# Two graph layers: layer 0 with values stationary in column halves of the array and masks in DRAM, layer 1 with queries on partitions

## The chip, the cores and the metric

The kernel runs on one core of a Trainium2 chip. Time is device microseconds of one execution; lower is better. A profiled execution gives the trace from which the views below are taken.

## The reference

x is 8 x 2048 x 256 in f32 and adj is 2048 x 2048 of 0 and 1, sparse and the same for all batches. Layer 0 is masked attention with 4 heads of 64, whose softmax runs inside each chunk of 256 keys by itself, so a query sums eight separate softmaxes:

```
h = relu(layernorm(x))
scores = clip(q k^T / sqrt(64), -10, 10);  scores = where(adj == 0, -10, scores)
attn = softmax(scores over the 256 keys of a chunk)
ctx = sum over the 8 chunks of attn @ v
x = x + layernorm(ctx @ Wo^T + bo + h) * gamma + beta
```

Layer 1 is graph attention with one head: the logit of a query n and a key m is a sum of two scalars through a leaky relu, and the softmax runs over all keys.

```
g = relu(layernorm(x)) @ W;  s = g @ a1;  d = g @ a2
e = leaky_relu(s[n] + d[m], 0.01);  e = where(adj == 0, -1e9, e)
x = x + relu(softmax(e over m) @ g)
```

All is f32. Because s[n] is the same for all keys of a query, the largest logit of a query follows from the largest d among its neighbours.

## The kernel before

The eight batches run one after the other, and all loops are unrolled. In each batch four blocks of 512 tokens (`nb`) are loaded, normalized, transposed and projected (`project_qkv`); q and k stay with features on partitions, v with tokens on partitions, and v has a column of ones after each head's 64 (L118). Then the four blocks of queries go through layer 0, and then layer 1 runs over the whole batch.

Layer 0, per query block: `logits` (L226) makes for a head pair `p` and a key tile `mt` of 128 keys the scores with keys on partitions. The two heads lie in the upper and lower 64 rows of the array. One instruction on VectorE (L236) clips and masks them, taking the lesser of the score and `bound` (an int8 mask of keys by queries that lies in SBUF), and ScalarE takes the exponential (L240). `mix` (L243) then takes 128 x 128 pieces of these exponentials as the stationary operand, and the 65 columns of v and ones as the moving one, so that a chunk's weighted values and their sum come out with queries on partitions; VectorE divides (L255, L263), and GpSimd adds the chunk to `ctx4` (L264). A pass of the loop is a head pair and a chunk (two key tiles); `mix` follows one pass behind `logits`.

At a block's end `finish_layer0` (L266) transposes the context, projects it, adds, normalizes and adds to x; `start_layer1` (L304) normalizes again, multiplies by W (with two more columns for s and d), and folds the block's d into `dmax`, the largest d among each query's neighbours, by 16 instructions on VectorE (L326) with a second mask, `far`, also in SBUF.

Layer 1 (L342) has keys on partitions: for each half of the queries and each key tile, ScalarE takes a relu of a row of s plus the key's d (L379), GpSimd adds a row (L382), ScalarE takes the exponential (L383), VectorE masks (L384), and TensorE multiplies by g with eight accumulators that fill all of PSUM (L388). VectorE and GpSimd finish the eight query tiles (L394 to L401), and the block is stored (L404).

PSUM has three tags with two buffers each: `ps_s` of two banks (logits), `ps_a` and `ps_m` of one. The order of the instructions on each engine is not the order of the program text: a planner sorts them by priority (the program order) among those that it takes to be ready, with costs of its own, and each engine then runs them in that fixed order. All transfers go through SyncE's queue.

Of the kernel before, what the change touches and what calls it, by code (L numbers as in the profile page):

```python
# [17 lines left out]
P = 128  # L18
EPS = 1e-5
HEADS = 4  # L20
# [4 lines left out]
TINY = 2.0 ** -60  # L25
FAR = 64.0

NEVER = 1e30
# [3 lines left out]
def gnn_two_layers(  # L32
# [27 lines left out]
    KT = CHUNK // P  # L60
    SC = float(DH) ** 0.5
    assert F == 256 and DH == 64 and N % NB == 0

    const = ctx.enter_context(tc.tile_pool(name="const", bufs=1))
    xpool = ctx.enter_context(tc.tile_pool(name="xpool", bufs=NNB))
# [42 lines left out]
    woT = const.tile([P, FC, F], F32, name="woT")  # L108

    w1s = const.tile([P, FC, F + 2], F32, name="w1s")  # L110
    ones = const.tile([P, 1], F32, name="ones")
    nc.gpsimd.memset(ones, 1.0)

    bound = const.tile([P, NT, N], I8, name="bound")

    far = const.tile([P, NT, N], I8, name="sign")

    v = const.tile([P, NT, HEADS, DH + 1], F32, name="v")  # L118
    g = const.tile([P, NT, F + 1], F32, name="g")
    nc.gpsimd.memset(v[:, :, :, DH:DH + 1], 1.0)  # L120
    nc.gpsimd.memset(g[:, :, F:F + 1], 1.0)

    with tc.tile_pool(name="setup", bufs=2) as setup:
# [10 lines left out]
        for t in range(NT):  # L134
            rows = setup.tile([P, N], I32, tag="rows", name="rows", bufs=3)
            nc.sync.dma_start(rows, adj[t * P:(t + 1) * P, :])
            z = setup.tile([P, N], BF16, tag="z", name="z")

            nc.vector.tensor_scalar(z, rows, 0.0, -2.0, op0=ALU.is_equal, op1=ALU.mult)
            nc.gpsimd.tensor_scalar(far[:, t, :], z, FAR / 2, 0.0, op0=ALU.mult, op1=ALU.add)  # L140
            for half in range(NT // 8):
                pt = ps.tile([P, 8, P], BF16, tag="m", name="ps_z")
                for k in range(8):
                    m = half * 8 + k
                    nc.tensor.transpose(pt[:, k, :], z[:, m * P:(m + 1) * P], ident_b)
                dst = bound[:, half * 8:(half + 1) * 8, t * P:(t + 1) * P]
                if half % 2 == 0:
                    nc.vector.tensor_scalar(dst, pt, CLIP * SC, CLIP * SC, op0=ALU.mult, op1=ALU.add)
                else:
                    nc.scalar.activation(dst, pt, AF.Copy, bias=CLIP * SC, scale=CLIP * SC)  # L150

    nc.sync.dma_start(w1s[:, :, 0:F], w1.rearrange("(c p) f -> p c f", p=P))
# [5 lines left out]
    for c in range(FC):  # L158
        for i, a_r in enumerate((a1_r, a2_r)):
            junk = work.tile([P, F], F32, tag="hn", name="junk", bufs=3)  # L160
            nc.vector.scalar_tensor_tensor(
                junk, w1s[:, c, 0:F], 1.0, a_r, op0=ALU.mult, op1=ALU.mult,
                accum_out=w1s[:, c, F + i:F + i + 1],
            )
# [61 lines left out]
    def logits(pool, q, k, p, nb, mt):  # L226
# [3 lines left out]
        for i in range(2):  # L230
# [4 lines left out]
        e = pool.tile([P, 2, NB], F32, tag="e", name="e", bufs=2 * KT)  # L235
        nc.vector.scalar_tensor_tensor(  # L236
            e, s, -CLIP * SC, bound[:, mt, cols][:, None, :].to_broadcast([P, 2, NB]),
# [5 lines left out]
    def mix(pool, es, ctx4, p, j):  # L243

        for t2 in range(TB // 2):
            a = ps_a()[:, 0:4 * (DH + 1)].rearrange("p (s d) -> p s d", s=4)
            for s in range(4):
                t, i = 2 * t2 + s // 2, s % 2
                for kt in range(KT):
                    nc.tensor.matmul(  # L250
                        a[:, s, :], es[kt][:, i, t * P:(t + 1) * P], v[:, j * KT + kt, 2 * p + i, :],
                        start=kt == 0, stop=kt == KT - 1,
                    )
            rz = small.tile([P, 4], F32, tag="rz", name="rz")
            nc.vector.reciprocal(rz, a[:, :, DH])  # L255
            dst = ctx4[:, 2 * t2:2 * t2 + 2, 2 * p:2 * p + 2, :]
            num = a[:, :, 0:DH].rearrange("p (t i) d -> p t i d", t=2)
            rzb = rz.rearrange("p (t i) -> p t i", t=2)[:, :, :, None].to_broadcast([P, 2, 2, DH])
            if j == 0:
                nc.vector.tensor_tensor(dst, num, rzb, op=ALU.mult)  # L260
            else:
                part = pool.tile([P, 2, 2, DH], F32, tag="part", name="part", bufs=2)
                nc.vector.tensor_tensor(part, num, rzb, op=ALU.mult)  # L263
                nc.gpsimd.tensor_tensor(dst, dst, part, op=ALU.add)  # L264

    def finish_layer0(pool, x4, rn0, ctx4):  # L266

        o4 = pool.tile([P, TB, F], F32, tag="ctx", name="o4", bufs=2)
        for t2 in range(TB // 2):
            pt = ps_m()  # L270
            for i in range(2):
                for c in range(FC):
                    k = i * FC + c
                    nc.tensor.transpose(
                        pt[:, k * P:(k + 1) * P],
                        ctx4[:, 2 * t2 + i, 2 * c:2 * c + 2, :].rearrange("p h d -> p (h d)"), ident,
                    )
            cT = work.tile([P, 2 * FC, P], F32, tag="cT", name="cT")
            nc.scalar.activation(cT.rearrange("p k n -> p (k n)"), pt, AF.Copy)
            pp = ps_m()  # L280
            for i in range(2):
                for c in range(FC):
                    nc.tensor.matmul(  # L283
                        pp[:, i * F:(i + 1) * F], cT[:, i * FC + c, :], woT[:, c, :],
# [19 lines left out]
    def start_layer1(x4, nb, sd, dmax):  # L304
        _, rn = norm_stats(x4)
        hT = normed_transposed(x4, rn)
        for t2 in range(TB // 2):
            pp = ps_s()
            for i in range(2):
                t = 2 * t2 + i  # L310
                for di in range(FC):
                    nc.tensor.matmul(  # L312
                        pp[:, i, 0:F + 2], hT[:, di, t * P:(t + 1) * P], w1s[:, di, :],
# [3 lines left out]
            nc.scalar.activation(g[:, t0:t0 + 2, 0:F], pp[:, :, 0:F], AF.Copy)  # L317
            nc.vector.tensor_copy(
                sd[:, :, t0:t0 + 2].rearrange("p s t -> p t s"), pp[:, :, F:F + 2]
            )  # L320

        far_d = work.tile([P, NB], F32, tag="far_d", name="far_d", bufs=1)
        spread(far_d, sd[:, 1, nb * TB:(nb + 1) * TB], TINY)
        for t in range(NT):
            junk = work.tile([P, NB], BF16, tag="junk", name="junk", bufs=1)
            nc.vector.tensor_tensor_reduce(  # L326
                junk, far[:, t, nb * NB:(nb + 1) * NB], far_d, 1.0,
                -2 * FAR if nb == 0 else dmax[:, t:t + 1], ALU.add, ALU.max, dmax[:, t:t + 1],
            )

    def spread(dst, col, scale=1.0):

        for c4 in range(col.shape[1] // 4):
            pt = ps_m()
            for i in range(4):
                t = 4 * c4 + i
                nc.tensor.transpose(
                    pt[:, i * P:(i + 1) * P], col[:, t:t + 1].to_broadcast([P, P]), ident
                )
            nc.scalar.activation(dst[:, c4 * 512:(c4 + 1) * 512], pt, AF.Copy, scale=scale)  # L340

    def layer1(pool, b, xs, sd, dmax):  # L342
        W = N // 2
        src, dst = sd[:, 0, :], sd[:, 1, :]
        s_r = pool.tile([P, N], F32, tag="s_r", name="s_r", bufs=1)
        spread(s_r, src)
        top = pool.tile([P, 3, NT], F32, tag="top", name="top", bufs=1)
        none, w, zm = (top[:, i, :] for i in range(3))

        part = pool.tile([P, 2, NT], F32, tag="part1", name="part1", bufs=1)  # L350
        low, high = part[:, 0, :], part[:, 1, :]
        nc.vector.tensor_scalar(low, dst, SLOPE, None, op0=ALU.mult)
        nc.vector.tensor_tensor(high, dst, low, op=ALU.subtract)
        w_r = pool.tile([P, N], F32, tag="w_r", name="w_r", bufs=1)
        nc.vector.tensor_scalar(none, dmax, -FAR / 2, None, op0=ALU.is_lt)
        nc.vector.scalar_tensor_tensor(zm, dmax, 1.0 / TINY, src, op0=ALU.mult, op1=ALU.add)
        nc.vector.scalar_tensor_tensor(zm, zm, SLOPE, zm, op0=ALU.mult, op1=ALU.max)
        nc.vector.scalar_tensor_tensor(w, src, SLOPE, zm, op0=ALU.mult, op1=ALU.subtract)

        nc.vector.scalar_tensor_tensor(w, none, -NEVER, w, op0=ALU.mult, op1=ALU.add)  # L360
        spread(w_r, w)

        pg = ps_m()
        for m in range(NT):
            nc.tensor.matmul(
                pg[:, 0:F + 1], ones.to_broadcast([P, P]), g[:, m, :], start=m == 0, stop=m == NT - 1
            )
        gsum = pool.tile([P, F + 1], F32, tag="gsum", name="gsum", bufs=1)
        nc.scalar.activation(gsum, pg[:, 0:F + 1], AF.Copy)  # L369
        for half in range(N // W):  # L370
            cols = slice(half * W, (half + 1) * W)
            accs = []
            for _ in range(2):
                two = ps_s()
                accs += [two[:, 0, 0:F + 1], two[:, 1, 0:F + 1]]
# [88 lines left out]
```

## Time and profile before

| | |
|---|---|
| three runs | 5951.31, 5952.5 and 5953.0 us, median 5952.5 |
| the profiled execution | 5953.0 us, its span 5951.2 us |
| busy: TensorE matmuls, its weight loads | 4897.3 us (82%), 3684.2 us (62%) |
| busy: VectorE, ScalarE, GpSimd | 3133.4 (53%), 2116.9 (36%), 1837.6 us (31%) |
| mean granted TensorE clock | 0.91 |
| HBM read, written | 35.65 MB, 16.78 MB |

A row of the groups reads: line, engine, operation, tile written and tiles read, shapes, count; then the busy time in us and the mean ns of one; then the idle time of the engine just before and what ended it. PE is TensorE's matmuls, PEld its weight loads, DVE is VectorE, ACT ScalarE, POOL GpSimd, SP SyncE. A matmul's recorded duration includes its way through the pipeline, so the distance from start to start is the better price.

### The profile page before, as it was taken

The page shows a single profiled execution, that of the slowest core. Times are in us where ns is not written, and L with a number is a line of the kernel's source. Part 1 is how long each engine was busy: PE and PEld are TensorE (multiplying, and loading weights), DVE is VectorE, ACT ScalarE, POOL GpSimd, SP SyncE. Part 2 cuts the span into 40 slices and gives each one's busy share as a digit, 9 for nine tenths or more (in the row PEclk, how much of TensorE's full clock was granted, in tenths as well). Part 3 has the DMA queues.
Part 4 walks back from the last instruction along what each step waited for, and adds up shares of the span by engine and source line. Part 5 has one row for each costly group of instructions (what it writes and reads, how often), then busy time and mean ns, then how long its engine had stood idle before and what let it go on. Part 6 is the DMA issues. An engine that isn't in the chain of part 4 may idle for free.

```text
span 5951.2 us, 70683 instructions
## 1 busy us (share of the span) xinstructions
PE 4897.3 (82%) x28304; PEld 3684.2 (62%) x28304; DVE 3133.4 (53%) x6245; ACT 2116.9 (36%) x2361; POOL 1837.6 (31%) x1626
## 2 busy tenths in 40 slices
PE   7888698886988779887798777987789877897877
PEld 4666566665666556665666656665566655665656
DVE  4556445554455544555445554455544556445563
ACT  3333343333333243333433334332343333432333
POOL 2222422224222242223522225123251222513235
PEclk7999899998999989998899988998899988998989
DMA  3000000000000000000000000000000000000000
GB/s 142 1 1 1 0 29 1 1 1 11 18 1 1 1 15 15 1 1 1 15 15 1 1 1 15 15 1 1 1 15 15 1 1 1 15 15 1 1 1 15
DMA packets 39191, 56.96 MB, mean 10 GB/s; under 512 B 2000, under 2 KB 36816, under 8 KB 36816
## 3 DMA queue, kind: packets, MB, share of 16 engines
q1 hardware_dynamic: 38864, 52.44, 2.6%
q8 instruction: 225, 3.69, 0.3%
q14 instruction: 102, 0.84, 0.0%
HBM read 35.65 MB, written 16.78 MB: 9 GB/s over the span
## 4 chain that ended last, share of the span: by engine, by line
PE 56%; POOL 16%; DVE 14%; issue 8%; ACT 6%; DMA 0%; POOLq 0%; SPq 0%; ACTq 0%; DVEq 0%
PE ps_a L250 27%; PE ps_s L231 14%; POOL e L382 9%; DVE junk L326 4%; PE ps_m L206 4%; ACT e L379 3%; DVE e L236 3%; PE ps_s L312 2%; PE ps_m L283 2%; PE ps_m L215 2%; PE ps_m L195 1%; DVE e L384 1%; POOL x L302 1%; POOL o L301 1%; POOL o L300 1%
## 5 line engine op out<-in xcount | busy, mean ns | idle before, releaser
L250 PEld LDWEIGHTS ps_a<-v,e 128*128 128x128 f32 x16384 | 1872.2, 192 | 391.8 <-issue 303.2
L250 PE MATMUL ps_a<-v,e 128*128 128x65 f32 x16384 | 1943.6, 276 | 11.2 <-DVE part L263 10.8
L240 ACT ACTIVATE e<-e 128x1024 f32<-128x1024 f32 x1024 | 1082.2, 1057 | 1706.7 <-DVE e L236 1677.3
L264 POOL TENSOR_TENSOR ctx<-ctx,part 128x256 f32<-128x256 f32 x896 | 666.1, 744 | 2923.6 <-DVE part L263 2923.6
L236 DVE SCALAR_TENSOR_TENSOR e<-ps_s,bound 128x1024 f32<-128x1024 f32 x1024 | 1215.6, 1219 | 185.9 <-PE ps_s L231 185.7
L231 PE MATMUL ps_s<-q,k 64*128 64x512 f32 x4096 | 1096.4, 619 | 33.5 <-DVE e L236 33.5
L382 POOL TENSOR_TENSOR e<-e,w_r 128x1024 f32<-128x1024 f32 x256 | 635.6, 2489 | 671.4 <-ACT e L379 449.4
L384 DVE SCALAR_TENSOR_TENSOR e<-bound,e 128x1024 f32<-128x1024 int8 x256 | 374.7, 1464 | 672.6 <-ACT e L383 667.3
L388 PE MATMUL ps_s<-g,e 128*128 128x257 f32 x2048 | 533.4, 405 | 154.8 <-DVE h L394 100.1
L195 PE MATMUL ps_m<-ident,hn 128*128 128x128 f32 x512 | 121.4, 384 | 588.5 <-ACT hn L185 551.5
L231 PEld LDWEIGHTS ps_s<-q,k 64*128 64x128 f32 x4096 | 362.7, 185 | 343.1 <-issue 133.1
L388 PEld LDWEIGHTS ps_s<-g,e 128*128 128x128 f32 x2048 | 405.3, 202 | 252.2 <-DVE h L394 109.1
L255 DVE RECIPROCAL rz<-ps_a 128x4 f32<-128x4 f32 x1024 | 183.2, 181 | 652.3 <-PE ps_a L250 652.3
L383 ACT ACTIVATE e<-e,part 128x1024 f32<-128x1024 f32 x256 | 293.9, 1148 | 583.0 <-POOL e L382 583.0
L195 PEld LDWEIGHTS ps_m<-ident,hn 128*128 128x128 f32 x512 | 70.0, 183 | 654.4 <-ACT hn L185 599.4
L263 DVE TENSOR_TENSOR part<-ps_a,rz 128x256 f32<-128x256 f32 x896 | 378.4, 424 | 85.5 <-DVE rz L255 2.7
L326 DVE CUSTOM_DVE_ANT_0 junk<-sign,far_d,dmax 128x512 bf16<-128x512 int8 x384 | 292.3, 761 | 33.7 <-ACT far_d L340 29.4
L379 ACT ACTIVATE e<-s_r,part 128x1024 f32<-128x1024 f32 x256 | 287.5, 1136 | 61.2 <-PE ps_m L388 61.2
L388 PE MATMUL ps_m<-g,e 128*128 128x257 f32 x1024 | 271.7, 387 | 40.5 <-ACT gsum L369 38.7
L388 PE MATMUL ps_a<-g,e 128*128 128x257 f32 x1024 | 268.2, 383 | 7.1 <-DVE h L394 7.1
L185 ACT ACTIVATE hn<-x,rn 128x256 f32<-128x256 f32 x128 | 66.4, 589 | 550.3 <-DVE rn L179 550.3
L388 PEld LDWEIGHTS ps_m<-g,e 128*128 128x128 f32 x1024 | 194.2, 192 | 75.7 <-ACT gsum L369 41.9
(88 smaller groups left out, 3490.9 us busy)
## 6 DMA issues: line engine op xcount, KB each, us to landing
rows<-in_adj_dram SPq DMA_DIRECT2D x16, 1024.0 KB, 5.3
x<-in_x_dram SPq DMA_DIRECT2D x32, 512.0 KB, 3.9
out_dram<-x SPq DMA_DIRECT2D x32, 512.0 KB, 3.0
raw<-in_L_gnn_Wq_dram SPq DMA_DIRECT2D x1, 256.0 KB, 4.5
raw<-in_L_gnn_Wk_dram SPq DMA_DIRECT2D x1, 256.0 KB, 4.8
raw<-in_L_gnn_Wv_dram SPq DMA_DIRECT2D x1, 256.0 KB, 6.3
raw<-in_L_gnn_Wo_dram SPq DMA_DIRECT2D x1, 256.0 KB, 6.1
w1s<-in_L_gnn_W_dram SPq DMA_DIRECT2D x1, 256.0 KB, 7.0
```

Of the source, the lines that this page charges most:

```text
L231: nc.tensor.matmul(s[:, i, :], k[p][i * DH:(i + 1) * DH, mt * P:(mt + 1) * P], q[p][i * DH:(i + 1) * DH, cols], start=True, stop=True,)
L236: nc.vector.scalar_tensor_tensor(e, s, -CLIP * SC, bound[:, mt, cols][:, None, :].to_broadcast([P, 2, NB]), op0=ALU.max, op1=ALU.min,)
L240: nc.scalar.activation(e, e, AF.Exp, scale=1.0 / SC)
L250: nc.tensor.matmul(a[:, s, :], es[kt][:, i, t * P:(t + 1) * P], v[:, j * KT + kt, 2 * p + i, :], start=kt == 0, stop=kt == KT - 1,)
L263: nc.vector.tensor_tensor(part, num, rzb, op=ALU.mult)
L264: nc.gpsimd.tensor_tensor(dst, dst, part, op=ALU.add)
L326: nc.vector.tensor_tensor_reduce(junk, far[:, t, nb * NB:(nb + 1) * NB], far_d, 1.0, -2 * FAR if nb == 0 else dmax[:, t:t + 1], ALU.add, A ...
L379: nc.scalar.activation(e, s_r[:, cols], AF.Relu, bias=high[:, m:m + 1], scale=1.0 - SLOPE)
L382: nc.gpsimd.tensor_tensor(e, e, w_r[:, cols], op=ALU.add)
L383: nc.scalar.activation(e, e, AF.Exp, bias=low[:, m:m + 1])
L384: nc.vector.scalar_tensor_tensor(e, bound[:, m, cols], 0.0, e, op0=ALU.is_gt, op1=ALU.mult)
L388: nc.tensor.matmul(accs[k], e[:, k * P:(k + 1) * P], g[:, m, :], start=m == 0, stop=m == NT - 1)
```

## The change

Both layers change, and so does the place of the masks.

Setup: `bound` is written to four DRAM tiles, one for each query block, and the second mask, now `signs` (+1 for a neighbour, -1 else), to sixteen, one for each query tile. The column of ones in v and the two additional columns of w1s go.

Layer 0: the loop over a query block goes over key tiles, both head pairs in each. The values are now the stationary operand (64 columns for a head) and the exponentials the moving one, 512 queries long, so the context comes out with features on partitions. The two heads of a pair lie in the two column halves of the array. The sums come from four further matmuls for each key tile, one for each head in a column quarter of 32, with a stationary operand `picks` of ones and zeros that puts each chunk's sums into its own rows of `z`. ScalarE copies a chunk's unnormalized context to `au`. After each half (four chunks), `normalize` copies the sums out, reshapes them through DRAM, takes reciprocals, spreads them to 64 partitions each through DRAM, multiplies, and adds the four chunks on GpSimd. Finishing a block, and layer 1's start for it, is deferred to key tile 6 of the next block (`late`).

Layer 1: queries are on partitions. For each query tile its sign row is loaded, d is masked (VectorE), its largest found (VectorE), two exponentials are taken (ScalarE, one for each slope) and the larger chosen (VectorE); then the tile is transposed in TensorE, copied from PSUM by ScalarE and VectorE, and multiplied by g. s and d come from VectorE (eight for each block).

The core of the diff:

```diff
-    bound = const.tile([P, NT, N], I8, name="bound")
-    far = const.tile([P, NT, N], I8, name="sign")
-    v = const.tile([P, NT, HEADS, DH + 1], F32, name="v")
+    bounds = [dram.tile([P, NT, NB], I8, name=f"bound{i}") for i in range(NNB)]
+    signs = [dram.tile([P, N], I8, name=f"sign{i}") for i in range(NT)]
+    v = const.tile([P, NT, HEADS, DH], F32, name="v")
+    picks = const.tile([P, HALF_J, 32], F32, name="picks")
+    nc.gpsimd.memset(picks, 0.0)
+    for j in range(HALF_J):
+        nc.gpsimd.memset(picks[:, j, j * JR:(j + 1) * JR], 1.0)
...
-        e = pool.tile([P, 2, NB], F32, tag="e", name="e", bufs=2 * KT)
+        e = pool.tile([P, 2, NB], F32, tag="e", name="e", bufs=5)
...
+    def mix(es, acc, z, au, mt):
+        j, kt = mt // KT, mt % KT
+        jj = j % HALF_J
+        for p in range(HEADS // 2):
+            for i in range(2):
+                nc.tensor.matmul(
+                    acc[p][i * DH:(i + 1) * DH, :], v[:, mt, 2 * p + i, :], es[p][:, i, :],
+                    start=kt == 0, stop=kt == KT - 1,
+                )
+        for h in range(HEADS):
+            nc.tensor.matmul(
+                z[32 * h:32 * h + 32, :], picks[:, jj, :], es[h // 2][:, h % 2, :],
+                start=jj == 0 and kt == 0, stop=jj == HALF_J - 1 and kt == KT - 1,
+            )
+        if kt == KT - 1:
+            for p in range(HEADS // 2):
+                nc.scalar.activation(au[p][:, jj, :], acc[p], AF.Copy)
+
+    def normalize(pool, z, au, ctxT, first):
+        zc = pool.tile([P, NB], F32, tag="zc", name="zc", bufs=1)
+        nc.scalar.activation(zc, z, AF.Copy)
+        rows = HEADS * HALF_J
+        C = P // rows
+        zr = pool.tile([P, NB // C], F32, tag="zr", name="zr", bufs=2)
+        zd = dram.tile([rows, NB], F32, tag="zd", name="zd", bufs=2)
+        nc.sync.dma_start(zd, zc[::JR, :])
+        nc.sync.dma_start(zr, zd.rearrange("r (c f) -> (r c) f", c=C))
+        nc.vector.reciprocal(zr, zr)
+        rd = dram.tile([rows, NB], F32, tag="rd", name="rd", bufs=2)
+        nc.sync.dma_start(rd.rearrange("r (c f) -> (r c) f", c=C), zr)
+        for p in range(HEADS // 2):
+            rb = pool.tile([P, HALF_J, NB], F32, tag="rb", name="rb", bufs=2)
+            for i in range(2):
...
+                nc.sync.dma_start(
+                    rb[i * DH:(i + 1) * DH].rearrange("p j n -> p (j n)"),
+                    src.partition_broadcast(DH),
+                )
+            a = au[p]
+            nc.vector.tensor_tensor(a, a, rb, op=ALU.mult)
+            nc.gpsimd.tensor_tensor(a[:, 0:2, :], a[:, 0:2, :], a[:, 2:4, :], op=ALU.add)
...
+        for t in range(NT):
+            src = sd[:, 0, t:t + 1]
+            sg = pool.tile([P, N], I8, tag="sg", name="sg", bufs=3)
+            nc.sync.dma_start(sg, signs[t])
+            d = pool.tile([P, N], F32, tag="d", name="d", bufs=2)
+            nc.vector.scalar_tensor_tensor(d, sg, BIG, dst, op0=ALU.mult, op1=ALU.min)
...
+            nc.vector.tensor_reduce(dmax, d, AX.X, ALU.max)
...
+            for half in range(2):
...
+                nc.scalar.activation(e1, d[:, cols], AF.Exp, bias=b1)
+                nc.scalar.activation(e2, d[:, cols], AF.Exp, bias=b2, scale=SLOPE)
+                nc.vector.tensor_tensor(e1, e1, e2, op=ALU.max)
+                pt = ps_s().rearrange("p a n -> p (a n)")
+                for k in range(8):
+                    nc.tensor.transpose(pt[:, k * P:(k + 1) * P], e1[:, k * P:(k + 1) * P], ident)
+                eT = pool.tile([P, HALF], F32, tag="eT", name="eT", bufs=2)
+                nc.scalar.activation(eT[:, 0:512], pt[:, 0:512], AF.Copy)
+                nc.vector.tensor_copy(eT[:, 512:], pt[:, 512:])
+                for k in range(8):
+                    m = half * 8 + k
+                    nc.tensor.matmul(
+                        acc, eT[:, k * P:(k + 1) * P], g[:, m, :], start=m == 0, stop=m == NT - 1
+                    )
...
             for nb in range(NNB):
...
+                bd = pool.tile([P, NT, NB], I8, tag="bd", name="bd", bufs=2)
+                nc.sync.dma_start(bd, bounds[nb])
+                for mt in range(NT + 1):
+                    if mt < NT:
+                        es = [logits(pool, q, k, bd, p, nb, mt) for p in range(HEADS // 2)]
+                    if ahead is not None:
...
+                        if m % (KT * HALF_J) == 0:
+                            z = ps_m()
+                            au = [
+                                pool.tile([P, HALF_J, NB], F32, tag="au", name="au", bufs=3)
+                                for _ in range(HEADS // 2)
+                            ]
+                        if m % KT == 0:
+                            acc = [ps_a() for _ in range(HEADS // 2)]
+                        mix(ahead, acc, z, au, m)
+                        if m % (KT * HALF_J) == KT * HALF_J - 1:
+                            normalize(pool, z, au, ctxT, half == 0)
+                    ahead = es
+                    if mt == 6 and late:
+                        late.pop()()
```

## The prediction

> **What bounds the kernel now.** I read the page first, then the busy time by stage, then the timeline inside each stage. On the page:
>
> ```profile
> span 5951.2 us, 70683 instructions
> ...
> L250 PEld LDWEIGHTS ps_a<-v,e 128*128 128x128 f32 x16384 | 1872.2, 192 | 391.8 <-issue 303.2
> L250 PE MATMUL ps_a<-v,e 128*128 128x65 f32 x16384 | 1943.6, 276 | 11.2 <-DVE part L263 10.8
> ...
> L231 PE MATMUL ps_s<-q,k 64*128 64x512 f32 x4096 | 1096.4, 619 | 33.5 <-DVE e L236 33.5
> ```
>
> An f32 matmul stands as two records, each with a weight load (1024 calls of logits give 4096). L250 is half of PE's work, and its busy time (1943.6) hardly exceeds that of its weight loads (1872.2): 65 moving columns do not pay for a 128x128 load. Busy time by stage, for batch 1 (start:end, length, then PE, PEld, DVE, ACT, POOL busy, clock, DMA share, GB/s):
>
> ```profile
> 809.00:862.00 53.00, 51.99 (x179) 28.90 (x179) 17.66 (x46) 22.79 (x36) 3.47 (x4) 0.93 0.09 30
> 862.00:973.00 111.00, 96.53 (x644) 73.29 (x642) 57.98 (x109) 34.14 (x35) 31.08 (x36) 0.96 0.00 1
> 973.00:1352.00 379.00, 316.92 (x2076) 238.27 (x2076) 224.52 (x471) 124.32 (x138) 98.46 (x111) 0.92 0.00 1
> 1352.00:1545.00 193.00, 144.08 (x612) 117.14 (x612) 87.79 (x153) 82.66 (x87) 94.31 (x52) 0.87 0.05 16
> ```
>
> These are: projections (53 us), first query block of layer 0, the other three (126.5 us each), layer 1 (193 us). Eight such batches and some 65 us of setup make the span. Timeline of steady layer 0:
>
> ```profile
> 944.39 1.99 PE L231 MATMUL ps_s<-q,k 64*128 64x512 f32 x8
> ...
> 946.31 3.65 PEld L250 LDWEIGHTS ps_a<-v,e 128*128 128x128 f32 x32 [0.76 <-issue]
> 946.31 3.79 PE L250 MATMUL ps_a<-v,e 128*128 128x65 f32 x32
> ```
>
> This repeats every 5.63 us without a hole: PE bounds it, and L250 takes 3.65 of the 5.63. 16 repeats are 90 us; the other 36 of a block are its end:
>
> ```profile
> 957.91 1.99 PE L283 MATMUL ps_m<-woT,cT 128*128 128x256 f32 x8 [0.69 <-ACT cT L279]
> ...
> 970.55 2.34 POOL L302 TENSOR_TENSOR x<-x,o 128x1024 f32<-128x1024 f32 x1
> ...
> 976.87 2.16 PE L195 MATMUL ps_m<-ident,hn 128*128 128x128 f32 x8 [16.96 <-ACT hn L185]
> ```
>
> PE stands still for 17 us behind a chain of DVE and POOL, comes back at half clock (0.72 in the stage 954 to 976), and then shares DVE with L326. Layer 1's steady part:
>
> ```profile
> 1432.40 1.15 ACT L383 ACTIVATE e<-e,part 128x1024 f32<-128x1024 f32 x1 [2.46 <-POOL e L382]
> ...
> 1433.46 1.13 ACT L379 ACTIVATE e<-s_r,part 128x1024 f32<-128x1024 f32 x1
> ...
> 1434.67 2.35 POOL L382 TENSOR_TENSOR e<-e,w_r 128x1024 f32<-128x1024 f32 x1 [2.30 <-ACT e L379]
> ```
>
> A ring ACT, POOL, ACT of 4.65 us per key tile and half; PE needs 16 records at 0.217 = 3.5.
>
> **What the Trainium skill says.** "TensorEngine Tiling (Array Packing)", section Tiling Modes: tiles work independently, and changing the mode drains TensorE. The trace agrees for row tiles: 8 records of two heads take 4 x 0.429, as one head alone would; and 5.63 - 32 x 0.1115 - 4 x 0.429 = 0.35 us is left for two changes of mode. "TensorE: Matmul & The Clock Gate", Part 3: three column tiles of 32 columns gave 2.38x, and matmuls run strictly in program order. No run here shows column tiles; strict order does not fit the overlap of L231's heads, each of which has two passes. Same page, Part 1: an idle PE falls to half clock; here gaps of 5.2 and 17 us were followed by low clock.
>
> **The change, part by part,** per batch unless said.
>
> *Layer 0, PE.* A key tile for all four heads costs 5.63 now. New: logits unchanged, 4 passes x 0.429 = 1.72. Values: four matmuls with 64 stationary columns and 512 moving, two heads side by side in the columns: 4 passes = 1.72 if the halves overlap, 3.43 if not. Sums: four with 32 columns each: 2 passes = 0.86 if all overlap, 3.43 if not. Three mode changes at 0.18: 0.54. Both ends: 4.83 and 9.1 us. I take 4.83, because the row tiles overlap in just this kind of f32 pair and the page gives column tiles a gain near their number. Weight loads hide: 107 ns beside a pass of 429.
>
> *Layer 0, the others.* Per key tile DVE keeps 2 x 1.22 (L236), loses L255 and L263 (1.21 per key tile), and gains per block four multiplies of 128x2048 (2.27 each by L384's rate, bounds 2.2 to 2.6): about 63 us a block with the block end, below PE's 77. ACT: exp 2.11, evictions 0.6, some 51 a block. POOL loses L264, gains some 17 a block. All stay beside PE's matmuls; were PE as fast as 3.9 us a key tile, DVE would be the bound and each of these would count.
>
> *The half's normalization.* zc copy 0.6, three small transfers at 2.1 (the 1 KB row), reciprocal 0.2, 1 MB spread 5.3 (rows' landing; 3.0 to 8 as ends), multiply 2.3, POOL 2.35 + 1.2, and some 2 of waits: 20 us until one of three au buffers is free again. Only one is spare: the next half needs the second after two key tiles (some 9 us), and its copy waits on ACT; the exps of later key tiles stand behind it, DVE and PE wait for those, and the ps_a buffer that it should free keeps PE from the next values. Five e buffers let PE run on some 7 us (logits, head pair 0, sums). I take 5 us lost per half, clock included (0 to 9): 40. All seven DMAs of a half stand in SP's order, with the bd load behind them; that one is needed only a block later.
>
> *Block ends.* Deferred to the next block's sixth key tile, the chain of 17 us and the low clock hide under its matmuls; what stays on PE is about 9 us (8 + 8 matmuls of 256 columns at 0.43, eight transposes) three times, 27. If z keeps one ps_m buffer too long, the hT of a block comes later, which nobody awaits except after block 3. L274, L279, L326 (16 x 0.84 on DVE) go; eight sums for sd on DVE come (8 x 0.5 = 4).
>
> Sum from the projections' end to the last mix: 4 x 16 x 4.83 + 27 + 40 + 4 filling = 380, against 92 + 3 x 126.5 = 471.
>
> *After the last mix.* Now 19 to x4 and 193: 212. New: normalization 20, output projection and norms 19, W1 and sd 16, dst, first d, reduce and exps 12: 67. Then 16 query tiles. DVE per tile: d 2.27, reduce 2.2 (not in the trace; an estimate at L384's rate, 1.1 to 2.4), four small ones 0.8, two max 2.4, two copies 1.38, end 0.55: 9.6. PE: 16 transposes at 0.11, 16 x 0.433: 8.7, plus waits for eT. ACT 5.7. DVE becomes the bound; with buffers of two to three I take 10.5 (9.4 to 12.5), 168. Sum 235, +23. The order is the planner's, so d of the next tile may go ahead of this one's end; if not, see rival 3. sign loads of 256 KB (3 us) are far ahead in three buffers.
>
> *Setup.* Masks go out to DRAM (16 x 256 KB, 4 x 1 MB) and bounds come back: +20 (0 to 40) once. The dropped w1s columns are nothing (1.8 us of DVE, once). w1's matmuls move to ps_m: no price, beside L236.
>
> Sum: 8 x (-91 + 23) + 20 = -524 against the profiled 5953.0 (span 5951.2 and 1.8 around it; the median, 5952.5, is 0.5 lower): **some 5430 us**.
>
> **The rivals.** (1) *Column tiles do not overlap.* Sums and values then take 16 passes in place of 6: +4.29 per key tile, 275 per batch, less the 40 of waits that it covers: 5430 + 8 x 235 = **7310, slower**. It decides from 10 passes per key tile on (68 + 40 us over 64 tiles is 1.7 us, four passes). For it: no trace of a column tile, and twice to four times the moving data at once. Against: L231.
> (2) *They overlap only in program order*: a head's second pass holds the next head's first. 5 passes for the values and 5 for the sums: +1.72, 110 - 40: **5990**, about no change, 5800 to 6400. For it: rows are shared by column tiles, while L231's heads had their own.
> (3) *Layer 1 goes in series*: DVE holds this tile's end before the next d; 15 us a tile (half of the 22 that the whole chain has) in place of 10.5: +72: **6010**. Against: the trace shows L274 ahead of older L250, so the planner moves work forward.
>
> **How the numbers follow.** Main forecast 0.50, own range 5100 to 5850 (T 4.65 to 5.2, waits 0 to 9, layer 1 9.6 to 12); rival 1 0.18; rival 2 0.22; rival 3 0.10. A measurement here tells 0.2% (12 us). Faster: 0.47 + 0.04 + 0.03 = 0.54; same 0.01 + 0.03; slower 0.02 + 0.15 + 0.18 + 0.07 = 0.42. The range 5100 to 6400 leaves out rival 1 and the tails.
>
> **What would show it.** Eight records of the values in about 1.8 us, eight of the sums in 1.0, a steady period near 4.8: right; 2.2 and 2.2: rival 2; 3.5 and 3.5: rival 1. A gap of PE after each half that ends with a release by POOL or by ACT's au copy: the wait on au. Layer 1 between 10 and 12 us per query tile with DVE over 80% busy: right; under 65%: rival 3. No 17 us gap except once per batch. The forecast is wrong if the period in layer 0 exceeds 6.2.

## The result: 0.7% slower, with TensorE as fast as forecast and waiting more

The changed kernel takes 5994.7 us (median of four runs, 5986.5 to 6001.8) against 5952.6; the ratio is 1.0071, with an interval of 1.0053 to 1.0088. Forecast were 5430 us. The number lies beside those of rivals 2 and 3 (5990 and 6010), but neither mechanism was there, as the trace shows.

The names of its lines: L233 logits, L238 clip and mask, L242 exponential, L254 values, L259 sums, L265 ScalarE's copy to `au`, L290 VectorE's multiply of `au` by the spread reciprocals `rb`, L291 to L296 GpSimd's adds of the chunks, L306 the output projection, L174 to L199 the normalizations and the transposes behind them. From the page after (columns as before):

```profile
L233 PE MATMUL ps_s<-q,k 64*128 64x512 f32 x4096 | 1216.6, 653 | 216.7 <-DVE e L238 216.6
L254 PE MATMUL ps_a<-e,v 128*64 128x512 f32 x4096 | 1152.6, 660 | 248.5 <-ACT au L265 248.5
...
L259 PE MATMUL ps_m<-e,picks 128*32 128x512 f32 x4096 | 598.3, 620 | 0.0
```

The old values (L250) were busy for 1943.6 us; new values and sums together for 1751. In exchange the matmuls of layer 0 now wait: 248.5 us for ScalarE's copies, and 216.7 us in front of the logits where it was 33.5. The steady part, from the timeline of the changed kernel (start, length, engine, line, tiles, records):

```profile
1135.81 1.99 PE L233 MATMUL ps_s<-q,k 64*128 64x512 f32 x8
1137.73 1.94 PE L254 MATMUL ps_a<-e,v 128*64 128x512 f32 x8
1139.60 1.06 PE L259 MATMUL ps_m<-e,picks 128*32 128x512 f32 x8
1140.59 1.13 PE L233 MATMUL ps_s<-q,k 64*128 64x512 f32 x4
```

From start to start a key tile takes 4.78 us (1135.81 to 1140.59), where 4.83 were forecast. Eight records of values in 1.94 us and eight of sums in 1.06 us: the column tiles overlap fully. The single records say it too: in the sums at 1139.60 the first passes of all four heads start within 0.02 us, and the second passes 0.45 us later. Busy time by stage of the changed kernel, batch 1 (start:end, length, PE, PEld, DVE, ACT, POOL busy, clock, DMA share, GB/s):

```profile
827.00:880.00 53.00, 51.41 (x160) 25.98 (x161) 14.05 (x30) 24.28 (x39) 1.09 (x2) 1.00 0.12 40
880.00:1026.00 146.00, 129.35 (x602) 38.79 (x600) 69.55 (x72) 62.52 (x76) 31.80 (x18) 0.96 0.16 38
1026.00:1367.00 341.00, 258.48 (x1068) 81.89 (x1068) 153.93 (x226) 122.37 (x157) 98.42 (x57) 0.83 0.20 44
1367.00:1564.00 197.00, 159.84 (x812) 133.35 (x812) 155.90 (x249) 91.42 (x109) 20.95 (x21) 0.93 0.12 39
```

The stages are projections, the first part of layer 0, its rest with the end of block 3, and layer 1. In the third the clock is 0.83, and TensorE is busy for 258 of 341 us in spite of that. Means over batches 1 to 6, read off the traces (us for one batch; "period" is the time from one batch to the next, "layer 0" runs from the start of the projections to the last logits, "block" from one block's last addition to x to the next one's, the mean of the first two such stretches; e1, e2, e6 and e7 are experiments below):

| kernel | period | layer 0 | block | last logits to end of layer 0 | layer 1 |
|---|---|---|---|---|---|
| before | 733.8 | 513.6 | 126 | 27.1 | 192.4 |
| forecast | 665.8 | 429 | 96 | | |
| after | 737.4 | 484.6 | 118 | 52.8 | 197.7 |
| e1 | 683.8 | 430.8 | 103 | 53.0 | 197.7 |
| e2 | 696.5 | 440.2 | 104 | 56.2 | 197.8 |
| e6 | 661.6 | 405.6 | 96 | | |
| e7 | 641.1 | 384.7 | 89 | 56.3 | 197.7 |

(The forecast's 429 is 53 + 380, less 4 for the last mix; its block is 16 x 4.83 + 9 + 2 x 5.) So the changed layer 0 gained 29 us a batch where some 85 were expected, and layer 0's end with layer 1 lost 31.

Three waits stand in a steady block. The first two come at a block's end, in the timeline of the changed kernel (in brackets: idle time before, and its releaser):

```profile
1099.40 2.29 DVE L290 TENSOR_TENSOR au<-au,rb 128x2048 f32<-128x2048 f32 x1 [4.57 <-DMA rb<-rd]
...
1102.88 1.18 PE L233 MATMUL ps_s<-q,k 64*128 64x512 f32 x4 [2.89 <-DVE e L238]
...
1105.62 3.19 POOL L296 TENSOR_TENSOR ctxT<-ctxT,au 128x512 f32<-128x512 f32 x1
...
1108.84 0.60 ACT L265 ACTIVATE au<-ps_a 128x512 f32<-128x512 f32 x1 [4.92 <-POOL ctxT L296]
...
1109.49 1.98 PE L254 MATMUL ps_a<-e,v 128*64 128x512 f32 x4 [5.42 <-ACT au L265]
```

**Wait A**: VectorE stands in its fixed order at L290 until `rb` has landed; the masks L238 of the next key tiles are queued behind it, and TensorE waits for them. **Wait B**: ScalarE stands at the copy to `au` until GpSimd's L296 has read the oldest of the three buffers; `ps_a` stays full, and TensorE stands at the next values. **Wait C** follows at the deferred start of layer 1:

```profile
1143.17 2.34 POOL L325 TENSOR_TENSOR x<-x,o 128x1024 f32<-128x1024 f32 x1
...
1145.54 0.75 DVE L174 BATCH_NORM_STATS2 stats<-x 128x6 f32<-128x256 f32 x2 [6.19 <-POOL x L325]
...
1147.08 1.19 DVE L238 SCALAR_TENSOR_TENSOR e<-ps_s,bd 128x1024 f32<-128x1024 f32 x1
1148.32 2.07 PE L233 MATMUL ps_s<-q,k 64*128 64x512 f32 x2 [6.60 <-DVE e L238]
```

The same chain through GpSimd as before, but now its end stands on VectorE in front of a mask that TensorE needs. From start to start of matmuls, the block has holes of 3.48, 6.06, 7.20 and 4.16 us, 20.9 in all. By the trace's record of the granted clock, half clock sets in still within the holes and lasts 10.2, 13.7 and 6.8 us; 20.7 us of it lie behind the holes' ends, which costs some 10. TensorE's idle time proper in the four holes, 18.5 us, and these 10 make up the 29 us by which a block is longer here than in e7 (118 for 89).

### The profile page after: what moved, and what is told of

Read it like the earlier page. It is cut to its first block, busy times and chain, and to the rows that moved or that the text cites. A ratio compares the mean times of both kernels' runs of the same rounds, so it can differ in the third digit from the quotient of the medians.

```text
span 5993.0 us, 54681 instructions
## 1 busy us (share of the span) xinstructions
PE 4841.2 (81%) x21392; PEld 2273.5 (38%) x21392; DVE 3201.1 (53%) x4645; ACT 2422.3 (40%) x3057; POOL 1238.2 (21%) x797
## 4 chain that ended last, share of the span: by engine, by line
PE 54%; DVE 18%; POOL 13%; DMA 7%; ACT 5%; issue 2%; SPq 0%; POOLq 0%; DVEq 0%; ACTq 0%
PE ps_a L254 13%; PE ps_s L233 12%; PE ps_a L389 10%; PE ps_m L259 6%; DMA rb<-rd 4%; PE ps_m L208 4%; DVE e L238 3%; DVE d L365 3%; POOL au L291 3%; DVE au L290 2%; PE ps_m L335 2%; DVE e L380 2%; DVE st L368 2%; PE ps_m L306 2%; PE ps_m L217 2%
## 5 line engine op out<-in xcount | busy, mean ns | idle before, releaser
L238 DVE SCALAR_TENSOR_TENSOR e<-ps_s,bd 128x1024 f32<-128x1024 f32 x1024 | 1215.8, 1218 | 1198.0 <-PE ps_s L233 1088.5
L242 ACT ACTIVATE e<-e 128x1024 f32<-128x1024 f32 x1024 | 1076.2, 1053 | 1371.1 <-DVE e L238 1359.9
L233 PE MATMUL ps_s<-q,k 64*128 64x512 f32 x4096 | 1216.6, 653 | 216.7 <-DVE e L238 216.6
L254 PE MATMUL ps_a<-e,v 128*64 128x512 f32 x4096 | 1152.6, 660 | 248.5 <-ACT au L265 248.5
L389 PE MATMUL ps_a<-g,eT 128*128 128x257 f32 x4096 | 958.8, 386 | 66.7 <-ACT eT L385 45.5
L389 PEld LDWEIGHTS ps_a<-g,eT 128*128 128x128 f32 x4096 | 761.2, 191 | 215.4 <-ACT eT L385 83.2
L291 POOL TENSOR_TENSOR au<-au 128x1024 f32<-128x1024 f32 x128 | 300.9, 2351 | 2524.7 <-DVE au L290 2429.3
L233 PEld LDWEIGHTS ps_s<-q,k 64*128 64x128 f32 x4096 | 389.8, 195 | 962.4 <-issue 619.2
L254 PEld LDWEIGHTS ps_a<-e,v 128*64 128x64 f32 x4096 | 266.2, 145 | 992.2 <-issue 640.0
L259 PE MATMUL ps_m<-e,picks 128*32 128x512 f32 x4096 | 598.3, 620 | 0.0
L265 ACT ACTIVATE au<-ps_a 128x512 f32<-128x512 f32 x512 | 297.3, 587 | 380.0 <-PE ps_a L254 162.9
L290 DVE TENSOR_TENSOR au<-au,rb 128x2048 f32<-128x2048 f32 x128 | 306.4, 2393 | 188.0 <-DMA rb<-rd 169.9
L380 DVE TENSOR_TENSOR e<-e,e 128x1024 f32<-128x1024 f32 x256 | 310.3, 1217 | 79.3 <-ACT e L379 79.3
L378 ACT ACTIVATE e<-d,st 128x1024 f32<-128x1024 f32 x256 | 291.6, 1139 | 112.5 <-DVE st L371 112.5
L306 PE MATMUL ps_m<-woT,ctxT 128*128 128x256 f32 x512 | 153.1, 451 | 207.1 <-POOL ctxT L296 207.1
L365 DVE SCALAR_TENSOR_TENSOR d<-sg,dst 128x2048 f32<-128x2048 int8 x128 | 312.8, 2449 | 9.6 <-ACT dst L359 9.6
L379 ACT ACTIVATE e<-d,st 128x1024 f32<-128x1024 f32 x256 | 291.5, 1139 | 0.0
```

Of the source, the lines that this page charges most:

```text
L233: nc.tensor.matmul(s[:, i, :], k[p][i * DH:(i + 1) * DH, mt * P:(mt + 1) * P], q[p][i * DH:(i + 1) * DH, cols], start=True, stop=True,)
L238: nc.vector.scalar_tensor_tensor(e, s, -CLIP * SC, bd[:, mt, :][:, None, :].to_broadcast([P, 2, NB]), op0=ALU.max, op1=ALU.min,)
L242: nc.scalar.activation(e, e, AF.Exp, scale=1.0 / SC)
L254: nc.tensor.matmul(acc[p][i * DH:(i + 1) * DH, :], v[:, mt, 2 * p + i, :], es[p][:, i, :], start=kt == 0, stop=kt == KT - 1,)
L259: nc.tensor.matmul(z[32 * h:32 * h + 32, :], picks[:, jj, :], es[h // 2][:, h % 2, :], start=jj == 0 and kt == 0, stop=jj == HALF_J - 1 an ...
L265: nc.scalar.activation(au[p][:, jj, :], acc[p], AF.Copy)
```

## The experiments

**Theory**: these waits of a fixed order, with the low clock behind them, hold what the forecast gave away. **Rivals**: the column tiles' overlap carries less than it seems; layer 1 is what costs; the holes are only covers, and another engine takes over when they go. Ratios are to the kernel before, with intervals; differences are to the changed kernel (5994.7) unless said.

**e1_au4: a fourth au buffer** (and `zc` in `rb`'s slots, for room):

```diff
-tag="au", name="au", bufs=3
+tag="au", name="au", bufs=4
-zc = pool.tile([P, NB], F32, tag="zc", name="zc", bufs=1)
+zc = pool.tile([P, NB], F32, tag="rb", name="zc", bufs=2)
```

> The changed kernel with four au buffers in place of three (to fit, zc takes a slot of rb's tag). Theory of the order (the column tiles are as fast as forecast, 4.78 us per key tile; what is lost per query block are waits of an engine's fixed order, each followed by a low clock): the copy of au on ScalarE no longer waits for GpSimd (L293 and L296), the gaps of 4.2 and 6.1 us in PE per block go with half of their 17 us of low clock, some 18 us x 32 blocks = 570, less what the wait of the multiply for rb takes over: 5450 to 5750 us. Rival (the transfers of the sums set the pace, so a wait removed comes back at the next consumer): within 1% of the changed kernel's 5995, that is 5935 to 6055.

Measured: 5563.3 us, 0.9347 (0.9333 to 0.9361): 431 us less, 54 a batch. The copy no longer waits for GpSimd; in e1's timeline TensorE itself releases it:

```profile
1010.71 0.60 ACT L265 ACTIVATE au<-ps_a 128x512 f32<-128x512 f32 x1 [1.22 <-PE ps_a L254]
```

What is left of TensorE's waits in e1, the two largest (waiting line <- line awaited: us in total, times, longest):

```profile
PE ps_m L306 <- POOL ctxT L296: 208.8, 16, 23.4
PE ps_s L233 <- DVE e L238: 200.1, 78, 6.7
```

The wait of L254 for ScalarE is gone, and the other waits are about what they were (207.1 and 216.6 in the changed kernel). One buffer was worth over ten times the whole loss of the change.

**e8_zc_only: the control**, with `zc` moved and `au` left at three buffers:

```diff
-zc = pool.tile([P, NB], F32, tag="zc", name="zc", bufs=1)
+zc = pool.tile([P, NB], F32, tag="rb", name="zc", bufs=2)
```

> The changed kernel with three au buffers, but zc in a slot of rb's tag as in e1_au4: the other half of e1_au4's edit by itself. If the fourth au buffer made e1_au4's gain, this stays within 1% of the changed kernel's 5995 (5935 to 6055). If the move of zc or the planner's new order made it, it comes near 5563.

Measured: 6000.8 us, 1.0082 (1.0067 to 1.0098). The move alone brings nothing; the buffer made e1's gain.

**e2_hold: layer 1's start held back** behind the mask of key tile 10, three `au` buffers (names shortened here and below):

```diff
 if mt == 6 and late:
-    late.pop()()              # finish_layer0, then start_layer1
+    late[0][0]()              # finish_layer0
+if mt == 10 and late:
+    with tc.issue_after(last_mask):
+        late.pop()[1]()       # start_layer1
```

> The changed kernel, with layer 1's start for a block traced at key tile 10 of the next block and its VectorE instructions queued behind the masking of that key tile; all else as it was. Theory of the order: the gap of 7.2 us (L174 waits for GpSimd's x, L238 stands behind it) and its 13.7 us at half clock go, in three blocks of a batch: some 14 x 24 = 340 us, 5600 to 5750. Rival (GpSimd's chain is needed then in any case, or PE has no work to fill the gap): 5940 to 6010.

Measured: 5689.2 us, 0.9561 (0.9544 to 0.9577): 306 us less, 38 a batch. In e2's timeline VectorE's statistics now start 3.6 us after the end of GpSimd's addition, and without a wait:

```profile
989.78 2.38 POOL L327 TENSOR_TENSOR x<-x,o 128x1024 f32<-128x1024 f32 x1
...
995.76 0.74 DVE L174 BATCH_NORM_STATS2 stats<-x 128x6 f32<-128x256 f32 x2
```

e2's waits of TensorE (its lines stand two later):

```profile
PE ps_a L256 <- ACT au L267: 164.1, 44, 6.8
...
PE ps_s L235 <- DVE e L240: 21.6, 18, 3.5
```

The wait for masks fell from 216.6 to 21.6 us. A block became 14.1 us shorter (118.2 to 104.1), though the hole was one of 7.2: with it went 10.1 us of half clock behind its end (some 5 lost), and the wait for the copies fell too, from 248.5 to 164.1. The edit does two things, tracing the start at key tile 10 and holding it back; no run takes them apart.

**e3_au4_defer: e1 with the reciprocal and the multiply put later**, behind the masks of a key tile one and four or five after the half's end:

```diff
+steps = normalize(pool, z, au, ctxT, half == 0)    # now stops twice
+due += [[1, steps], [4 + half, steps]]
...
+with tc.issue_after(last_mask):
+    next(steps, None)
```

> Four au buffers as in e1_au4, and the reciprocal and the multiply of a half are queued on VectorE behind the masking of the first and of the fourth or fifth key tile after the half's end. Theory of the order: the multiply no longer stands in front of L238 while its rb is on the way; the gap of 3.5 us per block goes too, so all that hangs on the normalization: 22 us x 32 = 710 in all, 5200 to 5450, and clearly below e1_au4. Rival (the transfers set the pace): no better than e1_au4 within 1%.

Measured: 5668.2 us, 0.9518 (0.9503 to 0.9534): 105 us worse than e1, and a miss. With four buffers the wait A that this was to take away was down to 1.7 us (the block of e1 at 950 to 1050), and a late multiply makes a late context. In e3's timeline TensorE stands at the output projection (here L313) until GpSimd has added the second head pair's context:

```profile
1063.69 1.26 POOL L303 TENSOR_TENSOR ctxT<-ctxT,au 128x512 f32<-128x512 f32 x1
1065.01 2.93 PE L313 MATMUL ps_m<-woT,ctxT 128*128 128x256 f32 x6 [2.98 <-POOL ctxT L303]
```

In e3's waits of TensorE, that wait has grown from e1's 208.8 us at 16 places; the 24 new ones are one for each block whose end is deferred:

```profile
PE ps_m L313 <- POOL ctxT L303: 280.1, 40, 23.4
```

**e4_all: e2 and e3 together**, with the diffs of both.

> e2_hold and e3_au4_defer together. Theory of the order: the two add up, a query block takes 86 to 92 us (16 x 4.78 and some 9 for the block's end) in place of 119, 4900 to 5150 us in all, and the clock inside layer 0 stays at 1.0. Rival (a new bound, VectorE at some 63 us per block or the transfers, comes forward): the sum of the two gains is missed by over a third, 5300 or more.

Measured: 5494.8 us, 0.9227 (0.9213 to 0.9241): on the rival's side of what was expected. The block is near 100 us, with e3's wait of L313 in it and, as in e2 (218.9 us, where the changed kernel has 161.9), one at the transposes L197; e4's waits of TensorE:

```profile
PE ps_m L313 <- POOL ctxT L303: 249.3, 40, 19.6
PE ps_m L197 <- ACT hn L187: 220.7, 72, 17.8
```

**e6_au4_hold: e1 and e2 together**, without e3's part.

> e1_au4 and e2_hold together, without the deferral of the multiply that made e3_au4_defer slower than e1_au4. Theory of the order: the gains add up (432 and 306 below the changed kernel): 5257, 5180 to 5330, a block 89 to 94 us. Rival (with one wait gone the other comes forward, as in e4_all): 5400 to 5500.

Measured: 5400.5 us, 0.9071 (0.9058 to 0.9085): 94 us better than e4, so e3's part costs here too, 70 above the upper end of what was expected and at the lower end of the rival's range. e6's timeline shows what was left in a block:

```profile
1043.32 1.58 ACT L187 ACTIVATE hn<-x,rn 128x256 f32<-128x256 f32 x3 [1.32 <-DVE rn L181]
1043.98 0.33 PE L197 MATMUL ps_m<-ident,hn 128*128 128x128 f32 x1 [1.80 <-ACT hn L187]
```

Wait C once more, an engine further on: TensorE has the transposes in front of logits, while `hn` is still on its way through VectorE and ScalarE. There are 24 such holes in e6, of 2.2 to 3.7 us from start to start; after 23 of them, not after the one shown, half clock followed for 3.4 to 10.2 us.

**e7_hold_all: e6 with the start of layer 1 behind finished work on three engines**, VectorE's mask of key tile 10, ScalarE's exponential of 11 and TensorE's logits of 12:

```diff
-if mt == 10 and late:
-    with tc.issue_after(last_mask):
+if mt == 12 and late:
+    with tc.issue_after(mask[10]), tc.issue_after(exp[11]), tc.issue_after(logits[12]):
```

> e6_au4_hold, with ScalarE's and TensorE's part of layer 1's start queued too, behind the exponentials of key tile 11 and the logits of key tile 12. Theory of the order: the 2.4 us in which TensorE stands before the transposes of hn (seen in e2_hold and e4_all) and its 6.8 us of low clock go, some 5 us x 24 = 120 below e6_au4_hold. Rival: what stands behind them in ScalarE's order waits in its place, within 30 us of e6_au4_hold.

Measured: 5234.6 us, 0.8795 (0.8782 to 0.8809): 166 us under e6, where 120 were expected, and 12% under the kernel before. The start is also traced two key tiles later; no run has that alone. One steady block of e7, as a stage:

```profile
1006.00:1096.00 90.00, 89.83 (x430) 28.76 (x430) 59.05 (x83) 48.81 (x63) 31.84 (x20) 1.00 0.23 49
```

TensorE is busy for all of it at full clock, and VectorE and ScalarE have a third and more to spare. e7's waits of TensorE:

```profile
PE ps_s L386 <- DVE e L383: 179.8, 56, 13.5
PE ps_m L309 <- POOL ctxT L299: 177.2, 16, 19.7
PE ps_m L197 <- ACT hn L187: 165.2, 24, 17.7
```

The long ones among these stand at the seam between the layers, once a batch; whether other matmuls could fill it was not tried. Between the first and the last logits of a batch, the sums of the two traces (means of batches 1 to 6) leave little room for another cause: TensorE is idle for 58.8 us in the changed kernel and for 2.3 in e7, and at work under half clock for 65.6 and 0 us (33 lost). That is 89 of the 100 us between the two.

**e9_one_half: e7 with the values of both heads in the lower column half**, so that they cannot overlap. The context is then the sum of two heads, so this kernel leaves out the separate context of each and serves for the time alone; ScalarE copies the lower half into both halves of `au` (not shown):

```diff
-acc[p][i * DH:(i + 1) * DH, :], v[:, mt, 2 * p + i, :], es[p][:, i, :],
-start=kt == 0, stop=kt == KT - 1,
+acc[p][0:DH, :], v[:, mt, 2 * p + i, :], es[p][:, i, :],
+start=kt == 0 and i == 0, stop=kt == KT - 1 and i == 1,
```

> e7_hold_all with the values of both heads of a pair in the same, lower column half of the array, so that they can't overlap; ScalarE copies that half twice. The context is a sum of two heads and not the reference's: this is left wrong for the sake of the time. If the overlap of the column halves is what makes the new layer 0 short: 4 passes of 0.429 us more per key tile, 110 us a batch, 5235 + 880 = 6115 (5900 to 6150, as slower tiles cover some waits; slower than the kernel before or about equal). Rival (something else sets the key tile's period, the overlap is worth little): 5235 to 5500.

Measured: 6066.3 us, 1.0192 (1.0175 to 1.0209): 832 us above e7. e9's timeline, beside that of the steady part above:

```profile
1002.47 1.99 PE L235 MATMUL ps_s<-q,k 64*128 64x512 f32 x8
1004.39 3.65 PE L257 MATMUL ps_a<-e,v 128*64 128x512 f32 x8
1007.97 1.06 PE L262 MATMUL ps_m<-e,picks 128*32 128x512 f32 x8
1008.97 1.99 PE L235 MATMUL ps_s<-q,k 64*128 64x512 f32 x8
```

The values take 3.65 in place of 1.94 us and the period is 6.50. 832 us over 512 key tiles is 1.63 for each: the overlap of two column halves carries nearly its full worth, four passes of 0.429 us (1.72). No run takes the overlap of the sums' four quarters away; for them there is the trace alone.

**e5_l1_alone: the kernel before, with the new layer 1 alone** (signs in SBUF; no fold of d):

```diff
-start_layer1(xs[nb], nb, sd, dmax)    # folds d into dmax (L326)
+start_layer1(xs[nb], nb, sd)
...
-layer1(pool, b, xs, sd, dmax)         # keys on partitions
+layer1(pool, b, xs, sd)               # queries on partitions; sg = far[:, t, :]
```

> The kernel before with the new layer 1 alone (queries on partitions, transposes, two exponentials), its second mask as +1/-1 still in SBUF, and without the instructions of dmax at the blocks' ends; layer 0 as before. What the change did to layer 1 by itself. From the changed kernel's trace: from x4 of the last block to the end of layer 1 197 us in place of 193, +32 in all; the 16 instructions of L326 per block (13 us of VectorE) go. If they held up the next block's first passes: some 6 us x 24 less, 5800 to 5880. If they were hidden: 5970 to 6000. Either way layer 1 is not where the expected 520 us went.

Measured: 5897.0 us, 0.9910 (0.9893 to 0.9926), 56 us under the kernel before and between the two expectations. Layer 1 takes 4.2 us a batch more (196.6 against 192.4), and the blocks lose 4 us each without L326. The new layer 1 is a small gain in the old surroundings and not where the time went.

## Why the prediction was wrong, step by step

**Right: what TensorE can do.** The period (4.78 for 4.83), the full overlap of column tiles, and the other engines' load. Without the waits the sum holds: e7 has 384.7 us in layer 0, where the forecast less its 40 for waits is 389. What the Trainium skill says of independent tiles ("TensorEngine Tiling (Array Packing)", Tiling Modes) is borne out, with 1.94 us for four heads' two passes each. Rival 2 had read the skill's sentence on strict program order ("TensorE: Matmul & The Clock Gate", Part 3) so that a head's second pass holds the next head's first; the starts of the sums' records rule that reading out. Whether the sentence itself fails stays open, as no trace shows in which order the passes stand in the instruction stream. Rivals 1 and 2 fall with that.

**Right: layer 1 and setup.** Query tiles took 10.3 us on average for 10.5; VectorE was busy for 156 of 197 us, 79%, and for 89% from the first tile's d to the last one's. Rival 3 (15 us) falls. Setup grew by 14 us for 20. After the last mix, 9 us a batch more than forecast (46 for 39 to the end of layer 0, from a normalization of 28 us for 20; the rest in layer 1).

**Right in kind, its chain too short: "20 us until one of three au buffers is free again", and "I take 5 us lost per half, clock included (0 to 9): 40."** A third buffer that ScalarE's copy awaits, with TensorE behind it, is what the trace shows. But from a half's last sums to GpSimd's last add for the first head pair it took 31.9 us after a block's first half and 23.5 after its second (means of all 32 blocks). The spread landed after 8.0 us, the upper end, not 5.3; the forecast reckoned with 1 MB, and the four transfers of a half are 2 MB. The last add took 3.19 us for 1.2. The price came out close all the same: the buffer gave 54 us a batch by itself (e1) and 36 with the start of layer 1 held back (from e2 to e6), 4.5 to 6.7 a half. Part of e1's gain is wait A, which the forecast did not name.

**Failed: "Deferred to the next block's sixth key tile, the chain of 17 us and the low clock hide under its matmuls."** The forecast put this cost at nothing: it named what covers the chain but not what is queued behind its waiting instructions. L174 stands in front of a mask on VectorE (e2: 38 us a batch), and behind that L197 in front of logits on TensorE (e7 against e6: 21 a batch). Work that comes in the middle of a saturated loop hides only if no engine of the loop waits at it.

The two together: e7's 760 us, 95 a batch, against 40 in the forecast. The gains of e1 and e2 do not add up (54 + 38 for 74 in e6), since each hole partly covers others; taken one after the other, e1, e6 and e7 gave 54, 20 and 21. So of the some 55 a batch too many, 14 are the buffer's wait and 41 the cover that failed; in the other order, e2 first, all is the cover's. **The sum closes**: the period was 71.6 us longer than forecast (737.4 for 665.8), 56 of it in layer 0, 9 after the last mix, the rest at the seams; 8 x 71.6, less 6 for the setup, is 567 on top of 5430, that is 5997 against 5994.7.

Two readings of the kernel before were off without bearing on this: L250 was 40% of TensorE's busy time (1943.6 of 4897.3 us), not half, and eight periods of 733.8 leave some 80 us for the setup and the end, not 65.

The chance of 0.54 for faster stood on a wait that stayed within its bounds of 0 to 9 us a half, and on a cover that the text had not examined for the order of the queues. That rivals 2 and 3 name nearly the measured time is chance.

## What to carry to other kernels

When a loop is tightened until one engine has no slack, go through every instruction that is put into it from outside, and ask on each engine what stands behind it and when its input lands; a hole of a few us costs more than itself, since half clock follows: here 56 us of idle time a batch brought another 33 in the clock. Count buffers from the write to the last read of the slowest chain: here one more was worth 431 us. Putting an instruction later helps only where its input is what is late; where its output is awaited (e3), it makes the next wait.

## What the runs showed of the hardware

- Column tiles of f32 overlapped in full: two halves 1.94 us for what took 3.65 in one half (e9), and four quarters of sums in 1.06, their first passes starting within 0.02 us.
- In the changed kernel all 100 holes of TensorE of 3.6 us and more from start to start that began at full clock brought half clock, 3.4 to 13.7 us for those up to 7.5; of 41 holes between 2.0 and 2.6 us 12 did. Before the transposes in e6, 2.2 to 3.7 us sufficed in 23 of 24 cases. In e7's steady block without holes the clock was 1.00.
- GpSimd's add of 128x512 (L293 of the changed kernel) took 3.2 to 3.35 us in the 31 places where it started behind VectorE's multiply of two SBUF operands: the rest of the multiply (2.1 to 2.2 us) and 1.1 more. In the 33 others it took 1.27, also in the one where the multiply ran beside it but had started later.
- The four spreads of a half, 512 KB each, landed after 8.0 us in the page's row of transfers of the changed kernel (count, KB each, median us):

```profile
rb<-rd SPq DMA_DIRECT2D x256, 512.0 KB, 8.0
```
